# Two graph layers in one kernel: layer 0 on bf16 signs of the adjacency with one 512-column operand, row values from the diagonal, two message tables and an epilogue in three chunks

## The chip, the cores and the metric

The kernel runs on one core of a Trainium2 chip. The metric is the device time of one execution in microseconds (us). The kernel before takes 554.85 us, the median of three runs (553.38 to 556.07). A profile of one execution shows a span from the first to the last recorded instruction; the device time is longer than that span.

The engines named below are TensorE (PE in the profile, with its weight loads as PEld), VectorE (DVE), ScalarE (ACT), GpSimd (POOL) and SyncE (SP), whose queue starts most DMA transfers.

## What is computed

There are N = 2708 nodes with D = 128 features. The adjacency matrix is sparse: each row has its diagonal entry and a few neighbours, and every nonzero of a row has the same value, one over the row's degree. The first rows are the dense ones (about a hundred nonzeros), the last rows have a handful.

```python
# layer 0
XW = mobius_matvec(W, X)                       # X @ W, norms, artanh, tanh
gamma = 2.0 / max(1.0 - sum(XW * XW), EPS)
nominator   = A @ (gamma * XW)
denominator = clamp_abs(A @ (gamma - 1.0))
two_mean = nominator / denominator
AXW = mobius_scalar_mul(A.sum(-1), mobius_scalar_mul(0.5, two_mean))
x = layernorm(x + expmap0(relu(logmap0(AXW))))
# layer 1
s, d = x @ msg_w[:, :D].T, x @ msg_w[:, D:].T
messages = gelu(s[:, None, :] + d[None, :, :] + msg_b)      # for all i, j
aggregated = einsum('ijd,ij->id', messages, A)
new = concat([x, aggregated]) @ upd_w.T + upd_b
h = gelu(new) + x
x = layernorm(x + layernorm(h) * ln_w + ln_b)
```

Since messages are weighted with A, only the nonzeros of A need a message. The kernel finds them on the chip, and a dense path (behind an If, not taken with these inputs) covers matrices that have more of them than it has room for.

## The kernel before

The rows are 22 blocks of 128 nodes. The host hands over the adjacency transposed and in blocks (`adj_t`), so that one block of rows is one transfer of 1.44 MB.

*Prologue (L240 to L277).* x is transposed on TensorE block by block (L247), multiplied with W (L250), and `y` is formed: gamma times XW, gamma minus 1, and a column of ones, 130 columns per block of nodes.

*Layer 0, a loop over the blocks (L349 to L366).* SyncE starts the transfer of `aT` (L351, three buffers). ScalarE forms the signs of `aT` in bf16, `sgn` (L353); GpSimd clears the block's own diagonal in it (L355). TensorE adds up 22 f32 matmuls of `aT` with `y` in PSUM (L360), and ScalarE copies the result to `nom` (L363). `keys(b)` multiplies the signs, block by block, with a diagonal matrix of bit keys `kd` (L287, bf16), so that each nonzero leaves a number that holds its column, and VectorE takes the eight largest of each segment (MAX8, L292). `extract(l)` (L295 to L347) makes of them a list of edges: the degree of each row (L301), a running sum over the rows by a triangular matmul (L303, L304), a scan (L321), the selection matrix `R` that maps 128 edges to their rows (L311), selection matmuls (L336), and from their result the column index `J` and the flat index `F` of each edge (L344, L345). The value of each edge is then fetched from the adjacency by an indirect DMA, one for 128 edges, into `V` (L347, issued by GpSimd through the helper at L164). There are 98 tiles of 128 edges.

*Epilogue and projection (L369 to L429).* For all 22 blocks at once: norms, artanh, tanh, relu, the residual and the layer norm, as operations on 22 columns or on 2816 elements per partition on VectorE. Then block by block x is transposed (L417), projected (L420), and the d half is written to a table in DRAM (L429).

*Messages (L431 to L511).* For each block and each four tiles: GpSimd gathers the rows d_j from the table by `J` (L494, through L164; `dd`, four buffers), TensorE forms s_i with `R` (L495) and transposes `R` (L496), VectorE multiplies the transposed `R` by `V` (L498) and adds s and d (L502), ScalarE applies gelu (L503), TensorE adds up the weighted messages in `ag` (L505). The edge of a node to itself comes in with `gd` and the diagonal `dg` (L483, L484). `update` (L455) and `finish` (L462: gelu, two layer norms; the power -1/2 at L438 and three elementwise operations at L469 to L471 are on GpSimd) run for groups of 4, 4, 4, 4, 3, 2 and 1 blocks.

*Flag (L514 to L540).* Counts are compared to decide whether the dense path is needed.

Each engine executes its instructions in program order, as the Tile framework has written them down from this loop; semaphores tie engines together. PSUM banks and SBUF tiles come from pools with a fixed number of buffers, and a tile is free again when its last reader is through.

Of the kernel before, what the change touches and what calls it, by code (L numbers as in the profile page):

```python
# [10 lines left out]
F32 = mybir.dt.float32  # L11
U32 = mybir.dt.uint32
# [6 lines left out]
P = 128  # L19
BALL_EPS = 1e-5  # L20
# [3 lines left out]
MAGIC = 1597463007.0  # L24

BANK = 4
SPLIT = [[16, 8, 8, 4, 4, 1]] + [[4, 1, 1, 1, 1, 1]] * 2 + [[2, 1, 1, 1, 1, 1]] * 6 + [[1] * 6] * 13  # L30
CUTS = [[(0, 1), (1, 3), (3, 6)]] + [[(0, 6)]] * 21
TILES = [8, 6, 5, 8, 7, 5, 5, 4, 4, 4, 4, 4, 3, 3, 4, 3, 3, 3, 3, 3, 3, 3, 2, 1]
KEY = 0x5000
SPAN = 8192.0


def lists():

    out, t, c = [], 0, 0
    for b, cuts in enumerate(CUTS):  # L40
        for k0, k1 in cuts:
            n = TILES[len(out)]
            w = 8 * sum(SPLIT[b][k0:k1])
            out.append((b, range(k0, k1), c, w, t, n))
            t += n
            c += w
    return out, t, c
# [3 lines left out]
def hyperbolic_then_message_kernel(  # L51
# [3 lines left out]
    adj: bass.AP,  # L55
    adj_t: bass.AP,
    adj_d: bass.AP,
    w0: bass.AP,
# [6 lines left out]
    table: bass.AP,  # L65
# [4 lines left out]
    assert D == P and N % 2 == 0  # L70
    NB = (N + P - 1) // P
    NP = NB * P
    rows = [min(P, N - b * P) for b in range(NB)]
    full = NB if rows[-1] == P else NB - 1
    LISTS, NT, NC = lists()
    CMAX = max(v[3] for v in LISTS)
    NL = len(LISTS)
    TMAX = max(TILES)
# [4 lines left out]
    ps = ctx.enter_context(tc.tile_pool(name="ps", bufs=2, space=bass.MemoryType.PSUM))  # L83


    ident = const.tile([P, P], F32, name="ident")
    make_identity(nc, ident)
    x_sb = big.tile([P, NB, D], F32, name="x_sb")
    if full < NB:
        nc.gpsimd.memset(x_sb[:, full, :], 0.0)  # L90
    nc.sync.dma_start(x_sb[:, :full, :], x[: full * P, :].rearrange("(b p) d -> p b d", p=P))
    if full < NB:
        nc.sync.dma_start(x_sb[: rows[-1], full, :], x[full * P :, :])
    w0_sb = const.tile([P, D], F32, name="w0_sb")
    nc.scalar.dma_start(w0_sb, w0)
    mw = const.tile([P, 2 * D], F32, name="mw")
    nc.scalar.dma_start(mw, msg_w)
    uw = const.tile([P, 2 * D], F32, name="uw")
    nc.scalar.dma_start(uw, upd_w)
    mb = const.tile([P, 1], F32, name="mb")  # L100
    nc.scalar.dma_start(mb, msg_b.rearrange("(p o) -> p o", o=1))
    dg = const.tile([P, NB], F32, name="dg")
    nc.scalar.dma_start(dg, adj_d)
    rowvec = {}
    for name, src in (("ub", upd_b), ("lw", ln_w), ("lb", ln_b), ("mbr", msg_b)):
        t = const.tile([P, D], F32, name=name)
        nc.scalar.dma_start(t, bass.AP(tensor=src.tensor, offset=src.offset, ap=[[0, P], [1, D]]))
        rowvec[name] = t

# [3 lines left out]
    nhalf = const.tile([P, 1], F32, name="nhalf")  # L113
    nc.gpsimd.memset(nhalf, -0.5)
# [7 lines left out]
    loose = dict(allow_small_or_imprecise_dtypes=True)  # L122
    iota = const.tile([P, TMAX * P], F32, name="iota")
    nc.gpsimd.iota(iota, pattern=[[1, TMAX * P]], base=0, channel_multiplier=0, **loose)

    place = const.tile([P, TMAX], F32, name="place")
    nc.gpsimd.iota(place, pattern=[[P, TMAX]], base=1, channel_multiplier=1, **loose)
    nc.gpsimd.tensor_scalar(place, place, SPAN, 4096.0, op0=OP.mult, op1=OP.add)

    first = const.tile([P, NB], F32, name="first")  # L130
    nc.gpsimd.iota(first, pattern=[[P, NB]], base=0, channel_multiplier=1, **loose)
    nc.gpsimd.tensor_scalar_mul(first, first, float(N))

    key = const.tile([P, NB], I32, name="key")
    nc.gpsimd.iota(key, pattern=[[P, NB]], base=KEY, channel_multiplier=1)
    nc.vector.tensor_scalar(key, key, 16, None, op0=OP.logical_shift_left)
    kd = const.tile([P, NB, P], BF16, name="kd")
    nc.gpsimd.affine_select(
        kd,
        key.bitcast(F32).unsqueeze(2).to_broadcast([P, NB, P]),  # L140
        pattern=[[0, NB], [-1, P]],
        compare_op=OP.is_equal,
        fill=0.0,
        base=0,
        channel_multiplier=1,
    )

    wT = const.tile([P, 4, D], F32, name="wT")
    R = big.tile([P, NT, P], F32, name="R")
    J = const.tile([P, NT], U32, name="J")  # L150
    F = const.tile([P, NT], U32, name="F")
    V = const.tile([P, NT], F32, name="V")
    top = const.tile([P, NC], F32, name="top")
    deg = const.tile([P, NL], F32, name="deg")
    oe = const.tile([P, NL, 2], F32, name="oe")
    signs = const.tile([P, NB], F32, name="signs")
    cap = const.tile([P, NL], F32, name="cap")
    for l, (*_, n) in enumerate(LISTS):
        nc.gpsimd.memset(cap[:, l : l + 1], float(n * P))

    of_block = {b: [l for l, v in enumerate(LISTS) if v[0] == b] for b in range(NB)}

    def gather(o, src, at):
        nc.gpsimd.indirect_dma_start(  # L164
            out=o, out_offset=None, in_=src, in_offset=bass.IndirectOffsetOnAxis(ap=at, axis=0)
        )

    xT = big.tile([P, NP], F32, name="xT")
    mx = big.tile([P, NB, D], F32, name="mx")
    y = big.tile([P, NB, D + 2], F32, name="y")  # L170
    nom = big.tile([P, NB, D + 2], F32, name="nom")

    def bc(t):
        return t.unsqueeze(2).to_broadcast([P, NB, D])


    count = [0]

    def cols():
        count[0] += 1  # L180
        return sc.tile([P, NB], F32, name=f"c{count[0]}")

    def root(ss, least):

        a, s, q, o = cols(), cols(), cols(), cols()
        nc.vector.tensor_scalar_max(a, ss, least)
        nc.scalar.activation(s, a, AF.Sqrt)
        nc.vector.reciprocal(q, s)
        nc.vector.tensor_mul(q, q, a)
        nc.vector.tensor_add(q, q, s)  # L190
        nc.vector.tensor_scalar_mul(o, q, 0.5)
        return o

    def norm_of(v, room):
        sq = room[:, :, :D]
        nc.vector.tensor_mul(sq, v, v)  # L196
        ss = cols()
        nc.vector.tensor_reduce(ss, sq, axis=AX.X, op=OP.add)  # L198
        return root(ss, MIN_NORM * MIN_NORM)

    def artanh(n):

        z, zz, p, a, b, o = cols(), cols(), cols(), cols(), cols(), cols()
        nc.vector.tensor_scalar_min(z, n, 1.0 - BALL_EPS)
        nc.vector.tensor_mul(zz, z, z)
        nc.vector.tensor_scalar(p, zz, 1.0 / 15, 1.0 / 13, op0=OP.mult, op1=OP.add)
        for k in (11, 9, 7, 5, 3, 1):
            nc.vector.tensor_mul(p, p, zz)
            nc.vector.tensor_scalar_add(p, p, 1.0 / k)
        nc.vector.tensor_mul(p, p, z)  # L210
        nc.vector.tensor_scalar(a, z, -1.0, 1.0, op0=OP.mult, op1=OP.add)
        nc.vector.reciprocal(a, a)
        nc.vector.scalar_tensor_tensor(b, z, 1.0, a, op0=OP.add, op1=OP.mult)
        nc.scalar.activation(b, b, AF.Ln)
        nc.vector.tensor_scalar_mul(b, b, 0.5)
        nc.vector.scalar_tensor_tensor(a, z, 0.25, b, op0=OP.is_ge, op1=OP.mult)
        nc.vector.scalar_tensor_tensor(o, z, 0.25, p, op0=OP.is_lt, op1=OP.mult)
        nc.vector.tensor_add(o, o, a)
        return o

    def quotient(a, b):
        o, q = cols(), cols()
        nc.vector.reciprocal(q, b)
        nc.vector.tensor_mul(o, a, q)
        return o

    def product(a, b):
        o = cols()
        nc.vector.tensor_mul(o, a, b)
        return o  # L230

    def tanh(a, scale=1.0):
        o = cols()
        nc.scalar.activation(o, a, AF.Tanh, scale=scale)
        return o

    def bank(name, bufs=2):
        return ps.tile([P, 512], F32, name=name, bufs=bufs)

    with tc.tile_pool(name="stream", bufs=2) as stream, tc.tile_pool(name="small", bufs=2) as small:  # L240

        if full < NB:
            nc.gpsimd.memset(mx[:, full, :], 0.0)
        for b in range(NB):
            n = rows[b]
            tp = bank("mp")
            nc.tensor.transpose(tp[:, :n], x_sb[:n, b, :], ident[:n, :n])  # L247
            nc.scalar.copy(xT[:, b * P : b * P + n], tp[:, :n])
            mp = bank("kx", 3)
            nc.tensor.matmul(mp[:n, :D], lhsT=xT[:, b * P : b * P + n], rhs=w0_sb, start=True, stop=True)  # L250
            nc.scalar.copy(mx[:n, b, :], mp[:n, :D])
# [97 lines left out]
        for b in range(NB):  # L349
# [15 lines left out]
            for l in of_block[b]:  # L365
                extract(l)  # L366
# [260 lines left out]
```

## Time and profile before

| what | value |
|---|---|
| device time, median of 3 runs | 554.85 us |
| span of the profiled execution | 497.6 us |
| TensorE busy | 322.7 us (65%) |
| VectorE busy | 298.5 us (60%) |
| GpSimd busy | 242.0 us (49%) |
| ScalarE busy | 157.9 us (32%) |
| indirect gathers (V and dd) | 98 and 98, 967 and 968 ns each |
| transfer of one `aT` (1408 KB), issue to landing | 6.2 us |

A line of the profile's groups has: line of the kernel and engine, operation, output and input names with shapes, count; then busy time in us and the mean of one in ns; then idle time of the engine just before these instructions, and what ended it. A line of the waits has: engine, name and line, what it waited for; the total in us, the number of times, the longest.

The page cuts the span into 40 slices of 12.4 us; each digit is the busy share of a slice in tenths:

```profile
PE   1681998999999999997000058566582657657700
DVE  2629486676867767767989983422240537545751
ACT  1953142536455355451260225311120112111200
POOL 3200077778556354343000000677777878787441
PEclk9999997999999999999555559778887779586955
```

Layer 0 is in slices 5 to 18, the epilogue and projection in 19 to 25, the messages after that.

### The profile page before, as it was taken

What the parts mean: (1) busy time and instruction counts of PE and PEld (TensorE: products, weight loads), DVE (VectorE), ACT (ScalarE), POOL (GpSimd) and SP (SyncE); (2) the same over time, 40 slices, a digit from 0 to 9 for tenths busy, and PEclk for the clock granted to TensorE, in tenths of its full rate; (3) what the DMA queues carried; (4) which work ended last, traced back from release to release, by engine and by line L of the source; (5) the groups of instructions that cost most, each with busy time, mean ns of one, the idle gap of its engine ahead of it and who ended that gap; (6) DMA issues with size and microseconds to landing.
All of it is one profiled execution on the core that took longest, in us unless ns stands there. A gap on an engine that the chain in (4) does not pass through costs nothing.

```text
span 497.6 us, 7268 instructions
## 1 busy us (share of the span) xinstructions
PE 322.7 (65%) x2506; PEld 298.9 (60%) x2506; DVE 298.5 (60%) x965; ACT 157.9 (32%) x321; POOL 242.0 (49%) x321
## 2 busy tenths in 40 slices
PE   1681998999999999997000058566582657657700
PEld 1560997999999999996000046465572656657500
DVE  2629486676867767767989983422240537545751
ACT  1953142536455355451260225311120112111200
POOL 3200077778556354343000000677777878787441
PEclk9999997999999999999555559778887779586955
DMA  8600333355545546500000002111211121212000
GB/s 261 246 1 1 113 123 118 118 174 185 224 151 201 212 148 226 204 32 0 1 0 0 0 22 84 45 54 53 53 51 53 35 71 32 68 30 57 23 28 3
DMA packets 17718, 43.54 MB, mean 87 GB/s; under 512 B 6180, under 2 KB 12620, under 8 KB 14860
## 3 DMA queue, kind: packets, MB, share of 16 engines
q1 hardware_dynamic: 10108, 35.94, 20.1%
q0 software_dynamic: 6272, 6.49, 5.5%
q10 hardware_dynamic: 1296, 0.60, 0.5%
q8 instruction: 21, 0.34, 0.3%
q14 instruction: 21, 0.17, 0.1%
HBM read 40.18 MB, written 2.83 MB: 86 GB/s over the span
## 4 chain that ended last, share of the span: by engine, by line
PE 41%; POOL 18%; DVE 18%; issue 8%; ACT 6%; DMA 5%; ACTq 1%; POOLq 0%; DVEq 0%
PE mp L360 22%; POOL dd L164 12%; PE sel L336 5%; PE kx L287 5%; DMA dd<-table_dram,J 4%; PE kx L420 3%; POOL rs L438 2%; ACT sgn L353 2%; DVE c L198 2%; PE kx L250 2%; POOL v L469 1%; POOL v L470 1%; DVE y L196 1%; DVE top L292 1%; PE sel L304 1%
## 5 line engine op out<-in xcount | busy, mean ns | idle before, releaser
L164 POOL DMA_INDIRECT dd<-table_dram,J x98 | 94.9, 968 | 94.8 <-DMA table_dram<-nom 66.4
L164 POOL DMA_INDIRECT V<-in_adj_dram,F x98 | 94.8, 967 | 93.6 <-DVE F L345 57.7
L360 PE MATMUL mp<-y,aT 128*128 128x130 f32 x968 | 134.3, 286 | 3.4 <-ACT sgn L353 3.4
L360 PEld LDWEIGHTS mp<-y,aT 128*128 128x128 f32 x968 | 120.1, 196 | 3.7 <-ACT sgn L353 3.7
L292 DVE MAX8 top<-kx 128x8 f32<-128x512 f32 (+4 forms) x179 | 85.5, 512 | 6.5 <-PE kx L287 6.3
L353 ACT ACTIVATE sgn<-aT 128x2816 bf16<-128x2816 f32 x22 | 56.1, 2552 | 67.1 <-PE kx L287 56.5
L287 PE MATMUL kx<-kd,sgn 128*128 128x128 bf16 x484 | 44.8, 225 | 9.5 <-DVE top L292 9.5
L495 PE MATMUL kx<-y,R 128*128 128x128 f32 x196 | 40.2, 326 | 7.0 <-DVE dd L502 6.1
L287 PEld LDWEIGHTS <-sgn 128*128 128x128 bf16 x484 | 36.4, 103 | 11.8 <-DVE top L292 9.2
L503 ACT ACTIVATE ge<-dd 128x512 f32<-128x512 f32 (+3 forms) x30 | 16.6, 552 | 79.9 <-DVE dd L502 64.9
L496 PE MATMUL kx<-ident,R 128*128 128x128 f32 x98 | 25.7, 323 | 22.8 <-DVE rw L498 15.0
L505 PE MATMUL ag<-rw,ge 128*128 128x128 f32 x196 | 35.3, 333 | 7.2 <-DVE dw L483 3.1
L495 PEld LDWEIGHTS kx<-y,R 128*128 128x128 f32 x196 | 34.3, 236 | 8.8 <-DVE dd L502 7.6
L417 PE MATMUL mp<-ident,x_sb 128*128 128x128 f32 x22 | 5.1, 317 | 50.3 <-DVE x_sb L413 50.3
L502 DVE TENSOR_TENSOR dd<-kx,dd 128x512 f32<-128x512 f32 (+3 forms) x30 | 17.5, 582 | 33.0 <-DMA dd<-table_dram,J 27.7
L505 PEld LDWEIGHTS ag<-rw,ge 128*128 128x128 f32 x196 | 31.6, 242 | 8.9 <-ACT ge L503 8.6
L417 PEld LDWEIGHTS mp<-ident,x_sb 128*128 128x128 f32 x22 | 3.5, 161 | 52.0 <-DVE x_sb L413 50.4
L336 PE MATMUL sel<-z,R 128*128 128x49 f32 (+3 forms) x196 | 28.0, 288 | 7.7 <-DVE R L311 4.5
L336 PEld LDWEIGHTS sel<-z,R 128*128 128x128 f32 x196 | 25.3, 202 | 9.2 <-issue 5.0
L496 PEld LDWEIGHTS kx<-ident,R 128*128 128x128 f32 x98 | 15.0, 168 | 25.0 <-DVE rw L498 15.9
L321 DVE TENSOR_TENSOR_SCAN scan<-m,oe 128x48 f32<-128x48 f32 (+3 forms) x24 | 8.8, 367 | 30.4 <-ACT oe L305 30.3
L458 PE MATMUL sel<-wT,xT 128*128 128x128 f32 x44 | 11.3, 351 | 19.0 <-DVE h L460 19.0
(165 smaller groups left out, 518.5 us busy)
## 6 DMA issues: line engine op xcount, KB each, us to landing
aT<-in_adj_t_dram SPq DMA_DIRECT2D x22, 1408.0 KB, 6.2
V<-in_adj_dram,F POOLq DMA_INDIRECT x98, 2.4
dd<-table_dram,J POOLq DMA_INDIRECT x98, 2.5
table_dram<-nom SPq DMA_DIRECT2D x22, 64.0 KB, 1.5
out_dram<-h SPq DMA_DIRECT2D x21, 64.0 KB, 1.6
mw<-in_L_gnn_msg_w_dram ACTq DMA_DIRECT2D x1, 128.0 KB
uw<-in_L_gnn_upd_w_dram ACTq DMA_DIRECT2D x1, 128.0 KB
w_sb<-in_L_gnn_W_dram ACTq DMA_DIRECT2D x1, 64.0 KB, 1.8
```

The costliest lines, as they stand in the source:

```text
L164: nc.gpsimd.indirect_dma_start(out=o, out_offset=None, in_=src, in_offset=bass.IndirectOffsetOnAxis(ap=at, axis=0))
L287: nc.tensor.matmul(kp[:, i * P : (i + 1) * P], lhsT=sgn[:, j, :], rhs=kd[:, j, :], start=True, stop=True)
L292: nc.vector.max(top[:, c : c + 8], seg[:, s, :])
L336: nc.tensor.matmul(sp[:, k, :], lhsT=R[:, t0 + k0 + k, :], rhs=z, start=True, stop=True)
L353: nc.scalar.activation(sgn, aT, AF.Sign, accum_out=signs[:, b : b + 1])
L360: nc.tensor.matmul(op[:, : D + 2], lhsT=aT[:, j, :], rhs=y[:, j, :], start=(j == 0), stop=(j == NB - 1))
L420: nc.tensor.matmul(dp[:, : 2 * D], lhsT=x1T[:, b * P : (b + 1) * P], rhs=wT[:, 0:2, :].rearrange("p a d -> p (a d)"), start=True, stop=True,)
L495: nc.tensor.matmul(X[:, k, :], lhsT=R[:, t, :], rhs=s_nm[:, b, :], start=True, stop=True)
L496: nc.tensor.transpose(RT[:, k, :], R[:, t, :], ident)
L502: nc.vector.tensor_tensor(dd[:, :w, :], X[:, :w, :], dd[:, :w, :], op=OP.add)
L503: nc.scalar.activation(ge[:, :w, :], dd[:, :w, :], AF.Gelu)
L505: nc.tensor.matmul(ag[:, :P], lhsT=ge[:, k, :], rhs=rw[:, k, :], start=False, stop=(k0 + k == t1 - 1))
```

## The change

Blocks have 124 rows now (22 x 124 = 2728). The three limbs of y (bf16 parts whose sum is y; 3 x 129 columns), a column of ones and 124 key columns (block j has the key 2^j) make one operand of 512 bf16 columns. One matmul for each pair of blocks, signs with this operand, gives sums, count and keys together. Since the nonzeros of a row all have the row's diagonal value, the sums of signs are scaled by the diagonal; that the values do equal the diagonal is counted on VectorE over the whole matrix. The gather of V is gone. The epilogue and the projection run in three chunks of blocks, after blocks 10, 19 and 21, and the messages are split by the half of the nodes from which they come: table 0 holds blocks 0 to 10, table 1 the others. All early messages (table 0) of all blocks come first, then the late ones with update and finish, in groups of two blocks. x arrives already transposed beside its normal layout. `layer0` is the sums, signs and the comparison of one block; `batch` is the list making of `extract` for several blocks at once (peeling the keys of a word one after another, MAX8, degrees, columns, triangular matmuls, scan, R, selection, J); `factors` is some 35 small operations on the columns of a chunk, one artanh among them; `power` and `gather` are on GpSimd. The `layer0` matmul with `nidentb` takes the block's own key away. The flag's counts and the dense path are adapted. Names with limbs: `hi`, `mid`, `lo`.

```diff
-SPLIT = [[16, 8, 8, 4, 4, 1]] + ...
-TILES = [8, 6, 5, 8, 7, ...]
+CUT = 11
+CHUNKS = [(0, 11), (11, 20), (20, 22)]
+BATCHES = [((0,), 0), ((1,), 8), ((2, 3, 4), 4), ((5, 6, 7, 8, 9), 2), ((10, 11, 12, 13), 2),
+           ((14, 15, 16, 17, 18), 1), ((19, 20, 21), 1)]
+EARLY = [5, 5, 4] + [6, 5, 4, 4, ...]
+LATE = [2, 2, 2] + [3, 2, 2, 2, ...]
...
+    def layer0(b, store):
+        dgb = stream.tile([Q, Q], F32, name="dgb", bufs=2)
+        nc.sync.dma_start(dgb, ...)
+        sgn = stream.tile([Q, NB, Q], BF16, name="sgn")
+        for h in range(2):
+            aT = stream.tile([Q, HALF, Q], F32, name="aT", bufs=3)
+            nc.sync.dma_start(aT, adj_t[b, :, h * HALF : (h + 1) * HALF, :])
+            at = 2 * b + h
+            nc.scalar.activation(sgn[:, ...], aT.bitcast(U32), AF.Sign, accum_out=nn[:, at : at + 1])
+            nc.vector.scalar_tensor_tensor(aT, aT, 1.0, dgb...to_broadcast([Q, HALF, Q]),
+                op0=OP.mult, op1=OP.is_equal, accum_out=ne[:, at : at + 1])
+        op = bank("op")
+        for j in range(NB):
+            nc.tensor.matmul(op[:Q, :WIDE], lhsT=sgn[:, j, :], rhs=ym[:, j, :], ...)
+            if j == 0:
+                nc.tensor.matmul(op[:Q, KEYS:WIDE], lhsT=nidentb[:Q, :Q], rhs=ym[:, b, KEYS:], ...)
+        nc.vector.tensor_reduce(nom[:, b, :], op[:Q, :ONES]..., axis=AX.X, op=OP.add)
+        nc.scalar.copy(cnt[:, b : b + 1], op[:Q, ONES : ONES + 1])
+        nc.scalar.activation(junk, nom[:, b, :D], AF.Square, accum_out=ss[:, b : b + 1])
...
+        for s, (lo, hi) in enumerate(segments(v.shape[2])):
+            nc.vector.max(v[:, i, s, :], words[:, lo:hi])
+            nc.vector.max_index(idx[:, i, s, :], v[:, i, s, :], words[:, lo:hi])
...
+    def peel(v, pid, keys, levels, shape):
+        for k in range(levels):
+            nc.vector.tensor_scalar(hi, v.bitcast(I32), 0x7F800000, None, op0=OP.bitwise_and)
+            nc.vector.tensor_tensor(keys(k), hi, pid, op=OP.bitwise_or)
+            if k + 1 < levels:
+                nc.vector.tensor_sub(v, v, hi.bitcast(F32))
...
+    def batch(blocks, S, v, idx):
...
+        limbs([zl[:, i]... for i in range(3)], scan, cmf)
...
+                nc.scalar.activation(r0[:, ...], iota[...], AF.Abs, scale=2.0, bias=mid[...])
+                nc.vector.tensor_scalar(R[:, t0 : t0 + nt, :]..., r0..., dflat..., -0.5, ...)
...
+                        nc.tensor.matmul(sp[:, q, :], lhsT=R[:, t, :], rhs=zl[:, h, k, i, :], ...)
+    def factors(b0, b1, dgc, den, cntc, ssc):
...
+    def epilogue(b0, b1, dgc, cntc, store):
+        f = factors(b0, b1, ...)
+        for b in range(b0, b1):
+            nc.scalar.activation(v, v, AF.Relu, scale=f[:, b - b0 : b - b0 + 1])
+            nc.scalar.activation(junk, v, AF.Square, accum_out=us[:, b : b + 1])
...
+        power(un, un, 0)                    
+        nc.scalar.activation(g, un, AF.Tanh)
...
+        for b in range(b0, b1):
+            nc.vector.scalar_tensor_tensor(v, v, g[...], x_sb[:, b, :], op0=OP.mult, op1=OP.add)
+            nc.vector.bn_stats(st, v)
+            nc.vector.bn_aggr(mv[:, b, :], st)
+        power(rs, rs, 1)
...
+        for b in range(b0, b1):
+            nc.scalar.activation(x_sb[:, b, :], nom[:, b, :D], AF.Identity, scale=rs..., bias=nm...)
+            nc.tensor.transpose(tp[:, :Q], x_sb[:, b, :], ident[:Q, :Q])
+            nc.scalar.copy(x1T, tp[:, :Q])
+            store(b, x1T)
+    def project(b, x1T):
+        dp = bank("op")
+        nc.tensor.matmul(dp[:Q, :], lhsT=x1T, rhs=wall..., start=True, stop=False)
+        nc.tensor.matmul(dp[:Q, :], lhsT=first3, rhs=bias..., start=False, stop=True)
+        nc.scalar.copy(d, dp[:Q, D : 2 * D])
+        nc.sync.dma_start(tables[k][at * Q : (at + 1) * Q, :], d)
+        limbs([sl[:, b, i, :] for i in range(3)], dp[:Q, :D], tmp)
+        nc.scalar.copy(own1[:, b, :], dp[:Q, 2 * D : 3 * D])
+        nc.scalar.activation(gd[:Q, b, :], dp[:Q, 3 * D :], AF.Gelu)
+    def messages(b, k):
...
+            dd = edge.tile([P, 4, D], F32, name="dd", bufs=3)
+                gather(dd[:, i, :], tables[k], J[:, t : t + 1])
+                for h in range(3):
+                    nc.tensor.matmul(X[:, i, :], lhsT=R[:, t, :], rhs=sl[:, b, h, :], ...)
+                nc.tensor.transpose(RT[:, i, :Q], R[:, t, :], identb[:Q, :Q])
+            nc.scalar.copy(rw[:, :w, :], RT[:, :w, :Q])
+            nc.vector.tensor_tensor(dd[:, :w, :], X[:, :w, :], dd[:, :w, :], op=OP.add)
+            nc.scalar.activation(ge[:, :w, :], dd[:, :w, :], AF.Gelu)
...
+        if k == 0:
+            nc.scalar.copy(gd[:, b, :Q], ag[:, :Q])
...
-        GROUPS = [(0, 4), (4, 4), (8, 4), (12, 4), (16, 3), (19, 2), (21, 1)]
+    for b in range(NB):
+        layer0(...)
+        if b in ends:
+            batch(blocks, S, v, idx)
+        for b0, b1 in CHUNKS:
+            if b == b1 - 1:
+                epilogue(b0, b1, dg, cnt, project)
+    for b in range(NB):
+        messages(b, 0)
...
+    GROUPS = [(b, min(2, NB - b)) for b in range(0, NB, 2)]
+    for b0, n in GROUPS:
+        for b in range(b0, b0 + n):
+            update(h[:, b - b0, :], messages(b, 1), b, dg[:, b : b + 1])
+        finish(h, b0, n)
```

Line numbers of the kernel after that the prediction uses: the comparison L352, the matmuls of layer 0 L363, the selection L492, the helper of the gathers L325.

## The prediction, made before the changed kernel ran

> **What bounds the kernel now.** I read the page's 40 slices first, then a table of stages, then the waits, then the chain that ended last. The table: stage from:to, its length, then busy time and instruction count of each engine, the granted clock, the DMA share and rate.
>
> ```profile
> 50.00:127.00 77.00, 73.83 (x661) 72.35 (x662) 51.42 (x162) 28.56 (x47) 49.90 (x64) 0.96 0.41 144
> 127.00:234.60 107.60, 104.96 (x1058) 103.16 (x1056) 78.33 (x235) 50.23 (x82) 52.97 (x76) 1.00 0.43 154
> 234.60:314.00 79.40, 21.59 (x96) 16.55 (x96) 65.58 (x223) 25.48 (x66) 0.94 (x1) 0.61 0.06 19
> 314.00:458.40 144.40, 89.13 (x541) 81.57 (x542) 58.51 (x183) 23.92 (x48) 113.72 (x114) 0.77 0.19 50
> ```
>
> Columns after the length are PE, PEld, DVE, ACT, POOL. Blocks 0 to 10, then 11 to 21 (layer 0): TensorE is full, 74 of 77 and 105 of 107.6 us; VectorE is at 67% and 73%. Then 79.4 us of epilogue and projection, alone on VectorE and ScalarE. Then the messages, where GpSimd has 114 of 144 us.
>
> ```profile
> POOL dd L164 <- DMA table_dram<-nom: 66.4, 1, 66.4
> ACT sgn L353 <- PE kx L287: 56.5, 16, 7.9
> POOL dd L164 <- issue: 23.5, 83, 0.3
> ```
>
> Line, whom it waited for, total, times, longest. The first message gather waits for the whole epilogue. The signs wait for matmuls, so ScalarE has slack in layer 0. From one gather to the next there is 0.3 us besides the gather itself, so a gather costs 1.25 us of GpSimd:
>
> ```profile
> L164 POOL DMA_INDIRECT dd<-table_dram,J x98 | 94.9, 968 | 94.8 <-DMA table_dram<-nom 66.4 <-issue 23.5 <-DMA dd<-table_dram,J 1.8
> L164 POOL DMA_INDIRECT V<-in_adj_dram,F x98 | 94.8, 967 | 93.6 <-DVE F L345 57.7 <-issue 20.9 <-DVE bad L515 12.4
> L438 POOL TENSOR_TENSOR rs<-ve,nhalf 128x4 f32<-128x4 f32 x8 | 8.4, 1047 | 3.9 <-DVE ve L448 3.8
> L438 POOL TENSOR_TENSOR rs<-ve,nhalf 128x2 f32<-128x2 f32 x2 | 1.4, 701 | 2.1 <-DVE tot L538 1.1 <-DVE ve L448 1.0
> L502 DVE TENSOR_TENSOR dd<-kx,dd 128x512 f32<-128x512 f32 x15 | 10.3, 687 | 26.3 <-DMA dd<-table_dram,J 20.9 <-PE sel L459 3.7 <-PE kx L495 0.8
> L292 DVE MAX8 top<-kx 128x8 f32<-128x512 f32 x97 | 65.1, 688 | 3.3 <-PE kx L287 3.1
> ```
>
> Of the two gathers of each tile, the V one already hides below TensorE. The page's chain agrees: PE 41%, POOL 18%, DVE 18%.
>
> [...] L287 issues 7 in 0.55 us and 4 in 0.39, 53 ns each; the granted clock is 0.61 in the epilogue. [...] I bound the pair with its maximum between one and three MAX8 passes (0.3 to 0.85 us at 128 columns, 285 ns measured for one) and take 0.4 for the mostly narrower segments.
>
> **The change part by part.** The profiled execution's span is 497.6 us; the median of the runs, 554.85, lies 57.2 above. I keep 57.2 around the new span.
>
> *Start.* The 22 transposes with their ScalarE copies (275 and 266 ns a pair) go; 12 limb copies and subtracts come (about 0.65 us each). Net shorter: I take block 0's sum complete at 46 us, against 57.3 now (first L360 at 50.0).
>
> *Layer 0, TensorE.* Out go 44 L360 instructions at 0.11 us (18 in 2.23, 4 in 0.67), the 22 key matmuls at 0.055, and a 49-column f32 selection: 7.5 us a block in the steady part (180.3 to 187.75). In come 22 [...] plus one small: 4.8 us, and 327 bf16 selection matmuls in all at about 0.06, some 20 us. TensorE alone would need 22 x 4.8 + 26 = 132 us instead of 185.
>
> *Layer 0, VectorE.* The added comparison with the diagonal (after's L352) is 44 passes of 1364 elements: [...] 1.58 us, plus 0.08 for the accumulator: 1.66 each, 73 us in all. A reduce of 387 adds 0.56 a block. The MAX8 of L292 (85.5 us on the page) are replaced by 46 pairs and by short MAX8 in the batches. For blocks 0 to 10: 20 compares 33, reduces 6, pairs 12, batch 0 with six peel levels and 31 MAX8 about 20 (small dependent operations follow each other at 0.215 us), batches 1 and 2 about 8.5 and 11: 91 us, and 6 of waits. In program order nothing covers it: the next batch of comparisons stands behind the batch chains on VectorE, and TensorE's queue has block 3's matmuls behind batch 0's selection. So 97 us, VectorE-bound: block 10 done at 46 + 97 = 143, while now block 10 is done at 127. Blocks 11 to 19: 3.3 + 0.6 + about 1.4 for pairs and the uncovered part of the batches = 5.3 a block, x9 = 48.
>
> *V gathers removed.* 98 x 1.25 us of GpSimd, all beside TensorE's layer 0: worth nothing by itself. Only where message gathers are put in their place does it pay. In the order of instructions only 12 of 109 stand before the end of layer 0, because dd has three buffers and the gelu that frees them stands on ScalarE after the last chunk.
>
> *Epilogue in 3 chunks.* ScalarE's queue has chunks 1 and 2 in one stretch without a Sign between, and the projection shares the two PSUM banks of layer 0's sums, so block 11's matmuls wait for almost all of chunk 1. The chunk is thus serial, not hidden. Chunk 1 (11 blocks): VectorE factors, about 35 small operations with the table load for Ln and the batch that is interleaved, 22; Relu and Square 11 x 0.59 = 6.5; pow (0.385 + 0.165 a column, from 1047 and 701 ns: 2.2) and tanh with its table load (1.3), 3.6 with what is small; multiply-add and statistics 11 x 0.49 = 5.4; second pow and two small operations 2.5; normalise, transpose, copy, project, four copies and gelu, ScalarE-bound, 11 x 1.7 + 3.5 = 22. Sum 62. Chunk 2 (9 blocks) by the same terms 54; blocks 20 and 21 then 10; chunk 3 to the first gelu of a message 17. The eleven table writes of chunk 1 stand on SP before a half block of 14; they are short (64 KB, 1.5 us) and cost a wait only if the halves are late.
>
> So layer 0 without chunks is 46 + 97 + 48 + 10 = 201, the chunks 133: messages run freely from 334 us, against 314 now.
>
> *Messages.* 62 early gathers remain: x 1.25 = 78, to 412. TensorE and VectorE have less to do than now (row value no longer multiplied in; R in bf16), so GpSimd is the pace. Late part: 35 gathers, and 11 groups each with two GpSimd adds (0.72 at 256 columns) and two pow at 0.70. h has two buffers, so a group starts when the one before last is through: about 10.2 us for two groups. 17 gathers and the first add 22; five pairs of groups 51; the last tail 9: 82, to 494. Last computation to span end is now 8.4; I take 7: 501. Dearest uncounted: the ring of three half blocks is held by the comparison[...]; I add 5% of the 150 us after block 0, 7. Span 508, time 508 + 57 = 565.
>
> Covers that could fail: the transfer of a half block (6.2 us for a whole one now, so about 3) is hidden by two halves in flight; if the comparison runs late on VectorE, each costs some 2 us, 44 in all up to 35 us, taken at 7. [...]
>
> **The rivals.**
>
> *Faster, 527.* One mechanism: VectorE's work of blocks 0 to 10 runs beside the batch chains' waits, because those chains stall on TensorE and ScalarE and comparisons fill the stalls. Layer 0 then goes at TensorE's 4.8 us plus selection, and blocks 0 to 10 take 70 us, not 97; chunk 1's factors fall beside the batch (-11). 565 - 27 - 11 = 527. For it: VectorE has 17 us idle at the scan L321 alone now. Against: the order on each queue is fixed, and 91 us are busy time, not waits. It decides if block 10 is done before about 116 us or the factors cost under 10.
>
> *No change, 555.* Same path, but the ring costs nothing (-7) and messages begin some 3 us earlier. A gain of layer 0 that exactly pays for the exposed chunks.
>
> *Much slower, 600.* The half-block ring turns into the bound: three buffers of half a block cover one and a half blocks only, against three whole ones now, and each is free only after the comparison. At 44 x 0.8 us exposed latency +35. For it: VectorE is behind by the batch chains. Against: 3 us a half is less than the work on it (2 x 1.66 per block beside 4.8).
>
> *Doing less than it says.* "Two tables" is to let gathers begin early, but with 12 of 74 placed in layer 0 only 15 us of GpSimd time is moved forward. That is inside the forecast.
>
> **How the numbers follow.** Forecast (565, own range 558 to 585) 0.45; much slower 0.20; no change 0.13; faster 0.22. About 0.5% (2.8 us) is what a measurement of this kernel can tell from none. The range 530 to 602 leaves out the lower half of the faster case and the upper half of the much slower one, 0.1 each. Faster 0.22, same 0.13, slower 0.65.
>
> **What would show it.** Comparison near 1.66 us x44; block 10's sums at about 143 us; a hole of some 50 to 60 us in TensorE's matmuls between blocks 10 and 11, another between 19 and 20; first free-running gathers near 334; gathers at 1.25 us after that; late part near 82. Wrong if the comparison is half as long, if Signs of block 11 run within chunk 1, or if the gathers start before 310.

## The result and the profile after

The kernel after takes 699.5 us (median of four runs, 698.6 to 700.6) against 555.3 us before: 1.262 times, interval 1.257 to 1.267. Forecast were 565 us, with 602 as the upper end of the range.

The page of the kernel after, its busy tenths and transfer rate in 40 slices of 17.4 us:

```profile
span 697.3 us, 6473 instructions
...
PE   4000827165771105854664410776655465676620
DVE  4247658464543643243443454245110111246551
ACT  2016423221512465531233144726222232343320
POOL 9100000000000212070000011004656646586641
...
DMA  5222111222222210142222210000211212121100
GB/s 144 87 104 103 57 69 45 101 85 103 105 98 105 103 72 7 35 98 102 105 103 103 98 46 0 22 12 19 51 37 43 46 30 47 38 54 31 30 24 17
```

The same two rows of the kernel before, in slices of 12.4 us, with layer 0 in slices 5 to 18:

```profile
DMA  8600333355545546500000002111211121212000
GB/s 261 246 1 1 113 123 118 118 174 185 224 151 201 212 148 226 204 32 0 1 0 0 0 22 84 45 54 53 53 51 53 35 71 32 68 30 57 23 28 3
```

In layer 0 of the kernel after (slices 5 to 23) no compute engine is full for long, while the transfer rate stands at 98 to 105 GB/s over whole stretches. Before, the same loop moved up to 226 GB/s in a slice. The DMA row says 2 tenths at the ceiling of the kernel after: about a quarter of the 16 engines' time, not all of it. So something limits the transfers that is not the engines' time in sum.

The groups of the kernel after, with count, busy time, mean in ns, idle time before and its releaser:

```profile
L363 PE MATMUL op<-ym,sgn 124*124 124x512 bf16 x484 | 140.9, 453 | 55.6 <-DVE idx L384 33.0 <-DVE hi L390 14.9 <-DVE m L429 6.5
L325 POOL DMA_INDIRECT dd<-table_dram,J x109 | 106.7, 979 | 87.7 <-ACT ge L613 29.2 <-issue 26.0 <-DMA table_dram<-d 25.3
L352 DVE SCALAR_TENSOR_TENSOR aT<-aT,dgb 124x1364 f32<-124x1364 f32 x44 | 69.3, 1574 | 102.5 <-ACT sgn L349 61.9 <-ACT cnt L373 40.7
L349 ACT ACTIVATE sgn<-aT 124x1364 bf16<-124x1364 uint32 x44 | 58.9, 1339 | 236.0 <-DMA aT<-in_adj_t_dram 210.3 <-issue 15.2 <-PE op L363 10.4
```

The signs (L349), which waited for matmuls before (56.5 us), now wait 210 us for the half blocks themselves, and the comparison (L352) waits for the signs. So the half blocks look like the cause and the comparison's wait like an echo; the experiments below test that. The comparison costs about what the prediction gave it, 1.574 us and 0.08 for the accumulator.

The stretches of the kernel after (from and to; length; busy PE, PEld, DVE, ACT, POOL; granted clock, DMA share, GB/s), cut where blocks 0, 10, 11, 19 had their sums, then at the first gelu of a message and at the first group's finish:

```profile
80.40:226.00 145.60, 74.99 (x398) 45.95 (x396) 80.11 (x307) 43.92 (x96) 1.65 (x6) 0.72 0.23 86
226.00:296.50 70.50, 27.50 (x143) 14.89 (x144) 30.36 (x155) 37.31 (x135) 10.28 (x8) 0.65 0.15 55
296.50:399.10 102.60, 55.93 (x230) 31.79 (x228) 41.04 (x120) 29.20 (x67) 13.30 (x14) 0.76 0.29 102
...
478.40:607.60 129.20, 74.73 (x555) 66.50 (x553) 20.20 (x57) 36.69 (x106) 76.25 (x81) 0.72 0.18 41
```

In the first and third line no engine has much more than half of the stretch, and 102 GB/s take 0.29 of the engines' time.

The kernel before takes 555 us in some sessions of measurement and 499 us in others, so each number below is marked kind 555 or kind 499 by what the kernel before took beside it, and numbers are compared within one kind. The profile before, with a span of 497.6 us, is of kind 499, while the timed runs beside it are of kind 555; in both kinds the device time is the recorded span plus 1.7 to 2 us. Some expectations below put the difference down to the chip. Both kinds were measured on chip number 3, so the chip alone doesn't make the kind.

### The profile page after: what moved, and what is told of

Read it like the earlier page. It is cut to its first block, busy times and chain, and to the rows that moved or that the text cites. A ratio compares the mean times of both kernels' runs of the same rounds, so it can differ in the third digit from the quotient of the medians.

```text
span 697.3 us, 6473 instructions
## 1 busy us (share of the span) xinstructions
PE 322.7 (46%) x1787; PEld 224.3 (32%) x1787; DVE 288.1 (41%) x1121; ACT 235.5 (34%) x677; POOL 177.8 (26%) x339
## 5 line engine op out<-in xcount | busy, mean ns | idle before, releaser
L363 PE MATMUL op<-ym,sgn 124*124 124x512 bf16 x484 | 140.9, 453 | 55.6 <-DVE idx L384 33.0
L349 ACT ACTIVATE sgn<-aT 124x1364 bf16<-124x1364 uint32 x44 | 58.9, 1339 | 236.0 <-DMA aT<-in_adj_t_dram 210.3
L325 POOL DMA_INDIRECT dd<-table_dram,J x109 | 106.7, 979 | 87.7 <-ACT ge L613 29.2
L352 DVE SCALAR_TENSOR_TENSOR aT<-aT,dgb 124x1364 f32<-124x1364 f32 x44 | 69.3, 1574 | 102.5 <-ACT sgn L349 61.9
L363 PEld LDWEIGHTS <-sgn 124*124 124x124 bf16 x484 | 75.6, 163 | 109.5 <-issue 71.2
L615 PE MATMUL ag<-rw,ge 128*128 128x124 f32 x218 | 47.2, 360 | 8.3 <-ACT rw L610 7.3
L605 PE MATMUL sel<-sl,R 124*128 124x128 bf16 x327 | 42.0, 273 | 9.9 <-DVE dd L612 9.4
L605 PEld LDWEIGHTS <-R 124*128 124x128 bf16 x327 | 32.2, 128 | 16.0 <-issue 14.7
L492 PE MATMUL sel<-zl,R 124*128 124x16 bf16 (+4 forms) x327 | 17.6, 197 | 33.8 <-ACT zl L298 12.7
L575 PE MATMUL op<-wall,x1T 128*124 128x512 f32 x44 | 29.4, 756 | 6.9 <-ACT x1T L569 6.8
L608 PE MATMUL rt<-identb,R 124*128 124x124 bf16 x109 | 22.1, 272 | 20.5 <-DVE R L476 8.9
L492 PEld LDWEIGHTS <-R 124*128 124x128 bf16 x327 | 15.5, 113 | 37.2 <-DVE R L476 29.1
L473 ACT ACTIVATE r<-iota,mid 124x256 f32<-124x256 f32 (+5 forms) x48 | 23.9, 531 | 3.1 <-DVE R L476 2.7
```

What stands on the lines that cost most here:

```text
L325: nc.gpsimd.indirect_dma_start(out=o, out_offset=None, in_=src, in_offset=bass.IndirectOffsetOnAxis(ap=at, axis=0))
L349: nc.scalar.activation(sgn[:, h * HALF : (h + 1) * HALF, :], aT.bitcast(U32), AF.Sign, accum_out=nn[:, at : at + 1])
L352: nc.vector.scalar_tensor_tensor(aT, aT, 1.0, dgb.unsqueeze(1).to_broadcast([Q, HALF, Q]), op0=OP.mult, op1=OP.is_equal, accum_out=ne[:, a ...
L363: nc.tensor.matmul(op[:Q, :WIDE], lhsT=sgn[:, j, :], rhs=ym[:, j, :], start=(j == 0), stop=(j == NB - 1))
L473: nc.scalar.activation(r0[:, : nt * P], iota[:Q, : nt * P], AF.Abs, scale=2.0, bias=mid[:, k * n + i : k * n + i + 1])
L492: nc.tensor.matmul(sp[:, q, :], lhsT=R[:, t, :], rhs=zl[:, h, k, i, :], start=(h == 0), stop=(h == 2))
```

## The experiments

### 128 partitions instead of 124

The profile's DMA share from block 11's sum to block 19's in the kernel after, 0.29 of 16 engines, is 4.6 engines' time on average, with the gathers in it. The traces don't name engines, but they have the start and the duration of each packet of a transfer, so that the packets in flight at one time can be counted. Transfers of 124, 125, 128 and of 112 and 12 partitions show how that count goes with the partitions.

`pad_at` and, in the other kind, `pad_at_again`:

```diff
-            aT = stream.tile([Q, HALF, Q], F32, name="aT", bufs=3)
-            nc.sync.dma_start(aT, adj_t[b, :, h * HALF : (h + 1) * HALF, :])
+            aT_all = stream.tile([P, HALF, Q], F32, name="aT", bufs=3)
+            nc.sync.dma_start(aT_all, adj_t[b, :, h * HALF : (h + 1) * HALF, :])
+            aT = aT_all[:Q]
```

with `adj_t` laid out with 128 rows per block, the last four of zeros.

> The kernel after, with one change: each half block of the adjacency is loaded as 128 partitions (four rows of zeros that nothing reads) instead of 124. Theory A (the 124-partition transfer uses few DMA engines and its rate bounds layer 0): a half block lands in about 3 us instead of 6 to 7, ScalarE's 210 us of waiting for aT nearly vanish, time 570 to 600 us. Rival B (the ring of three halves, held by the comparison, sets the pace): the transfers start no earlier, time above 680 us. Rival C (VectorE's batch chains set the pace, the waits for aT are only their echo): above 670 us.

> The kernel after, unchanged, beside the other three of this call on one chip. The loss against the kernel before in the same call: if the transfers' engines are the cause on any chip, after_again is 120 to 150 us slower than pad_at_again, whatever the kernel before takes here.

> pad_at once more, beside after_again and the kernel before. 120 to 150 us below after_again. On a chip where the kernel before takes 555 us: 1.03 of it. On one where it takes 500 us: 1.08 to 1.10 of it, since the kernel before lost 55 us on the other chips and the kernel after, whose layer 0 has other waits, less.

Measured: 572.0 us (kind 555; 1.031 of before, interval 1.027 to 1.036). In kind 499: after_again 669.3 and pad_at_again 542.5 us (1.088 of before). The padding is worth 127.5 us in one kind and 126.8 in the other. It costs 3% more bytes. ScalarE's wait for half blocks fell from 210 to 75 us in pad_at, less far than "nearly vanish". Of theory A it holds that the rate of the 124-partition transfers bounds layer 0; on how many DMA engines they run is not shown. B and C as the main cause fall.

`after_125` pads to 125 rows, `after_112_12` adds no byte:

```diff
-            nc.sync.dma_start(aT, adj_t[b, :, h * HALF : (h + 1) * HALF, :])
+            nc.sync.dma_start(aT[:112], adj_t[b, :112, h * HALF : (h + 1) * HALF, :])
+            nc.sync.dma_start(aT[112:], adj_t[b, 112:, h * HALF : (h + 1) * HALF, :])
```

> The kernel after, with each half block loaded as 125 partitions (one row of zeros that nothing reads). Theory A [...]: a quarter more rate, a half block in about 5.2 us instead of 6.5, time 625 to 660 us, between 699.5 and pad_at's 572. If it is the alignment of the rows, or a size that 128 happens to meet, 125 partitions do not help: above 690 us.

> The kernel after, each half block loaded by two transfers, 112 partitions and 12, without a byte added. Theory A: [...] as pad_at, 565 to 585 us. If it is the number of partitions in all that counts, 690 us or more.

Measured, both in kind 499: 630.5 and 546.5 us, against 669.3 with 124 partitions and 542.5 with 128. One row more gives 39 us. The prices of both expectations were worked out from the 699.5 and 572 us of kind 555; that 125 partitions would give a quarter more rate and 112 with 12 as much as 128 was the author's estimate. Against kind 499 the order is what they had right: 125 partitions lie between 124 and 128, and 112 with 12 is as fast as 128. From block 0's sum to block 10's it took 146.3 us with 124, 126.7 with 125, 90.3 with 112 and 12, 90.5 with 128.

The packets settle it. Of the time from block 11's sum to block 19's in which SyncE's queue has any packet in flight, it has four during 84% in the kernel after, and five during 81% in after_125. In pad_x_again (128 partitions, below) the number goes up to 16 and a few more. A packet (one partition's 5456 bytes) takes the same in all three, a median of 211, 211 and 209 ns. In after_112_12 the number goes as high as with 128 partitions, though a packet takes a median of 312 ns there. Four such packets at a time are 4 x 5456 bytes in 211 ns, or 103 GB/s, and five are 129 GB/s; the pages show 102 to 105 and 123 to 133. So with 124, 125 and 128 partitions the number of partitions changes how many packets go at once, and not how fast each one goes. In layer 0 of the profile before (128 partitions, 11264 bytes each) 16 are in flight during 50% of such time, more often than any other number. Why it is four, five and 16 is not shown.

`before_124` puts the cost into the kernel before:

```diff
-            nc.sync.dma_start(aT, adj_t[b])
+            nc.sync.dma_start(aT[:124], adj_t[b, :124])
+            nc.sync.dma_start(aT[124:], adj_t[b, 124:])
```

> The kernel before with each transfer of a block split in two, 124 partitions and 4 partitions. Theory A: the transfer of a block takes about 12 to 13 us instead of 6.2, and layer 0 goes at that pace (22 x 12.8 = 282 us instead of 185): time 635 to 665 us. Rivals B and C: below 565 us, since nothing else is changed. It also shows how the recorded span of a kernel of this form stands to its device time (497.6 and 554.85 us in the profile before).

Measured, kind 555: 629.0 us in the fastest of four runs, 638.8 to 642.0 in the others. The fastest is 73 us above the kernel before (555.8) and 6 us below the forecast range. The page of its profile stands at 100 to 108 GB/s over most of layer 0, again with four packets in flight, each of 11264 bytes and 424 ns (422 in the profile before). So the kernel before slows down by the same cause, without any other part of the change.

### What the comparison and the diagonal's transfer add

> The kernel after with 124-partition transfers, without the comparison with the diagonal on VectorE and without the transfer of the diagonal (the check that all values of a row equal its diagonal is left out). A half block is then freed by ScalarE alone and VectorE has 73 us less. Theory A: transfers stay at their rate, time 685 to 700 us. Rival B: 620 to 650 us. Rival C: 630 to 660 us.

> The kernel after with 124-partition transfers, where VectorE compares with a constant tile instead of the diagonal, so that the 22 small transfers of the diagonal are gone and the comparison's time stays (the check of the values is left out; its count is not used). after_no_compare was 34 us faster than after, with blocks 0 to 10 in 123.7 us instead of 145.7. If the transfers of the diagonal on the same few engines cost that, blocks 0 to 10 take 123 to 128 us here; if the comparison does, by holding a half block's buffer, 140 to 146 us.

The first removes L352 and the transfer at L343, the second only the transfer (`dgb = ones[:Q, :Q]`). Measured: after_no_compare 665.4 us (kind 555), 34 less than the kernel after and in none of the three ranges; after_compare_constant 654.4 (one run, kind 499), 15 less than after_again. Theory A had allowed 15 for leaving out the comparison, so this is a miss: transfers of 124 partitions are not all. From block 0 to 10: 145.6 us with both (146.3 in after_again), 139.2 with the comparison alone, 123.7 with neither, or 6.2 us for each of 20 half blocks. So of 22 us in this stretch about 15.5 are the comparison and 6.4 the diagonal's transfer in the same queue. What SyncE's queue waits for at the transfer of a half block, first in after_no_compare, then in after_compare_constant:

```profile
SPq L345 <- DMA aT<-in_adj_t_dram: 170.8, 34, 11.5
```

```profile
SPq L346 <- DVE aT L351: 85.1, 12, 24.6
```

Without the comparison, a transfer waits for an earlier transfer; with it, it waits for the comparison (L351 there), which holds the buffer until VectorE gets to it. So rival B exists, with a share of this size.

> The kernel with 128-partition half blocks, without the comparison and the transfer of the diagonal (the check of the values is left out). If VectorE's comparison is the next bound of layer 0, as the prediction has it, it is 40 to 73 us faster than with the comparison: 515 to 550 us. If TensorE or the batch chains are the next bound, it is less than 15 us faster.

With 128 partitions, leaving both out gives 533.8 us (kind 555), 38 less than pad_at (0.959 of before, interval 0.954 to 0.964), just below the forecast of 40 though inside the range of times. The 22 transfers of the diagonal are gone here too, so at most half of the comparison's 73 us stands in the path.

### The start, the writes and the chunks

`pad_x_and_diagonal` loads x and the diagonal as 128 partitions too; `pad_x_again` repeats it; `pad_writes_split` also splits each table write into 112 and 12 rows.

```diff
-    x_sb = big.tile([Q, NB, D], F32, name="x_sb")
-    nc.sync.dma_start(x_sb, x_p)
+    x_sb_all = big.tile([P, NB, D], F32, name="x_sb")
+    nc.sync.dma_start(x_sb_all, x_p)
+    x_sb = x_sb_all[:Q]
...
-        dgb = stream.tile([Q, Q], F32, name="dgb", bufs=2)
+        dgb_all = stream.tile([P, Q], F32, name="dgb", bufs=2)
...
```

> As pad_at, and x and the diagonal of each block are loaded as 128 partitions too. Theory A: x then lands some 15 us earlier, block 0's sums are complete near 55 us instead of 69, and the 22 small transfers take less of the queue: 550 to 562 us. If the start is set by the chain of small operations on VectorE instead, less than 5 us is gained.

> pad_x_and_diagonal once more: 20 to 28 us below pad_at_again on any chip (546 of 572 before).

> As pad_x_and_diagonal, with each write of the table as two transfers, 112 rows and 12. If the slow writes hold up the copies in the projection (their buffer is free only when the write has landed), the chunks get shorter by up to 10 us. If not, the extra transfers on SyncE cost 0 to 3 us.

Measured: 546.4 us in kind 555, 25.6 less than pad_at and below the forecast range of 550 to 562, and 0.988 of the kernel before (interval 0.984 to 0.991); 520.1 in kind 499, 22.4 less than pad_at_again, and 1.043 of before. In kind 499 block 0's sum comes at 50.6 us instead of 71.3, and blocks 0 to 10 take 87.8 us instead of 90.5, so that most of the gain is x at the start. Splitting the writes: 520.7 in kind 499, no difference.

`pad_one_chunk` is pad_at with `CHUNKS = [(0, 22)]`; `pad_all_one_chunk` is the same on pad_x_and_diagonal, and `pad_one_chunk_again` repeats that one.

> As pad_at, with one chunk of 22 blocks after layer 0 instead of three. The three chunks stand with some 128 us in the trace of pad_at (65, 50 and 13.5). If they are serial and each pays its fixed chain again, one chunk costs about 100 us by the prediction's terms, and the 12 early gathers that now stand among layer 0 (15 us of GpSimd) move behind it: 545 to 562 us. If the chunks pay by letting messages begin early, it is slower than pad_at, above 575 us.

> As pad_x_and_diagonal, with one chunk of 22 blocks. If the gain of one chunk (14 us at pad_at) is independent of the start, 528 to 540 us, faster than pad_x_and_diagonal's 546.4 and than the kernel before. If the transfers of the start gave the chunks room that one chunk doesn't have, no gain.

> pad_all_one_chunk once more: 10 to 30 us below pad_x_again, and below the kernel before on either kind of chip.

Measured: pad_one_chunk 557.7 us in kind 555, 14 less than pad_at and 1.008 of the kernel before; pad_all_one_chunk and its repeat 493.3 and 492.1 us in kind 499, 27 to 28 less than pad_x_again, and 0.987 and 0.988 of the kernel before (interval of the repeat 0.983 to 0.993). The range of 528 to 540 was meant for kind 555, in which this version was not run. The stretch from block 21's sum to the first gelu in pad_one_chunk_again, and the two chunk stretches with blocks in between in pad_x_again (columns as above):

```profile
214.00:295.60 81.60, 28.72 (x128) 14.89 (x125) 32.14 (x178) 46.17 (x194) 18.99 (x11) 0.69 0.06 16
```

```profile
138.40:205.00 66.60, 27.12 (x143) 14.84 (x144) 30.38 (x155) 37.44 (x135) 10.33 (x8) 0.67 0.17 53
205.00:254.90 49.90, 42.66 (x230) 25.82 (x228) 40.67 (x120) 28.90 (x67) 16.36 (x14) 0.97 0.77 225
254.90:327.70 72.80, 33.32 (x198) 20.39 (x199) 36.63 (x213) 39.81 (x139) 6.49 (x6) 0.70 0.05 16
```

One chunk of 22 blocks takes 82 us, less than the 100 expected; chunk 1 of 11 blocks alone takes 67 us, up to the next block's sum, so half the blocks don't cost half the time: each chunk pays a fixed chain again. The middle line is layer 0 as it was meant: 225 GB/s, VectorE 41 of 50 us, TensorE 43.

### More buffers for the gathered rows

> As pad_one_chunk, with eleven buffers for the gathered rows (in the memory of the 512-column operand, which is free after layer 0) instead of three. If the three buffers pace the early messages (125 us for 62 gathers in the trace, where 1.25 us each gives 78), that part falls to 80 to 95 us and the time is 30 us or more below pad_one_chunk. If the chain of TensorE, ScalarE and VectorE for each group of tiles paces them, less than 10 us is gained.

```diff
-            dd = edge.tile([P, 4, D], F32, name="dd", bufs=3)
+            dd = wide[:, ring[0] % 11 * 4 * D : (ring[0] % 11 + 1) * 4 * D].rearrange(...)
```

Measured: 562.0 us (kind 555) against 557.7: no gain. The waits for the gelu that frees a buffer were not the pace. Kind 499 shows what is. The messages of table 0 and the first two blocks of table 1 (79 gathers, up to the first group's finish) in pad_x_again and, of the same instructions, in after_again:

```profile
327.70:428.10 100.40, 70.21 (x562) 61.19 (x560) 20.16 (x58) 36.19 (x109) 76.27 (x81) 0.83 0.23 53
```

```profile
478.40:578.70 100.30, 73.15 (x565) 63.55 (x564) 20.09 (x58) 35.99 (x108) 76.24 (x81) 0.80 0.23 53
```

In 100 us there are 76 us of gathers with 0.3 us between them: 1.25 us each without a hole, so GpSimd is the pace and three buffers are enough. The kernel after, in kind 555, took 129 us for it (the last line of its stretches above) with the same busy time. The traces show where the holes begin. The last packet of a gather ends 2.2 us after the gather's start in both kinds (medians of after and after_again). But VectorE's addition, which needs the gathered rows, starts 0.5 us after that packet in after_again and 2.6 us after it in the kernel after (medians of the additions in this stretch; 0.5 us in pad_x_again and 2.9 in pad_x_and_diagonal). So in kind 555 the rows arrive as early after their gather starts, and the engine that uses them goes on later. What holds it up is not shown.

### The kernel before, once more

> The kernel before, unchanged, profiled once more. The profile before had a span of 497.6 us at a mean clock of 0.836, while the spans of the timed runs are 552 to 557 us at 0.79 to 0.81. If that profiled execution was an unusual one, the span is now 552 to 558 us, and the stage that is longer tells where the 55 us lie; a lower granted clock alone would make layer 0 longer and leave the messages, which GpSimd paces, as they were.

Measured: 555.4 us, span 553.7. Layer 0 and the messages are longer, the epilogue not (83.4 us in both from block 21's sum to the first message gather). A lower clock alone is thus not the cause, since by the expectation it would have left the messages as they were. One stretch of layer 0, in the profile before and in before_again:

```profile
97.90:142.00 44.10, 43.94 (x444) 43.16 (x442) 32.13 (x96) 20.68 (x34) 31.22 (x44) 1.00 0.52 180
```

```profile
97.90:142.00 44.10, 32.36 (x253) 30.25 (x253) 19.28 (x54) 13.29 (x23) 23.81 (x32) 0.85 0.29 99
```

The same 44 us hold 444 matmuls in one and 253 in the other. Block 21's sum is copied at 230.6 and at 265.3 us, the first message gather starts at 314 and 348.7: 35 us in layer 0, 31 of them by block 9, and the remaining 21 in the messages and what follows them. So the profile from which the prediction was worked out is not an unusual execution but one of kind 499.

## Why the prediction was wrong

Its points, beside the kernel after and beside the kernel whose large loads have 128 partitions (both kind 499, like the profile that the prediction was worked out from), in us from the span's start:

| point | prediction | after_again | pad_x_again |
|---|---|---|---|
| block 0's sum | 46 | 80.7 | 50.6 |
| block 10's sum | 143 | 227.0 | 138.4 |
| block 19's sum | 253 | 400.0 | 254.9 |
| block 21's sum | 317 | 465.4 | 314.3 |
| first gelu of a message | 334 | 478.4 | 327.8 |
| first group's finish (412 + 22) | 434 | 578.7 | 428.1 |
| last computation | 494 | 656.8 | 506.1 |
| span | 508 | 668.2 | 517.6 |

- The step that failed stands under "Covers that could fail": a half block's transfer "(6.2 us for a whole one now, so about 3) is hidden by two halves in flight". It carried the duration over from 128 partitions to 124. With 124 a half takes 6.2 us where nothing else holds it (after_no_compare), with the comparison and the diagonal's transfer 7.3 (145.6 us for 20), against 4.4 us of work (87.8 us for the same 20 in pad_x_again). A transfer of 124 partitions had four packets in flight where one of 128 had up to 16 and more. The place of the "much slower" rival was right and its price, 35 us, was not: it priced an exposed latency, where the rate had fallen. 127 us are shown for the half blocks and 22 to 26 for x and the diagonal. The prediction also priced this delay in two ways: 2 us for each of 44 would be 88 us, and its 35 us are 0.8 us for each.
- The diff had the number 124 in every tile, and the prediction asked of the transfers only whether they were hidden.
- "I keep 57.2 around the new span" was wrong as well. Around every span there are 1.7 to 2 us; the 57 were the difference between the two kinds. The kernel after, with no V gathers in layer 0, is about 30 us longer in kind 555 (669.3 to 699.5), not 57, and 29 of these lie in the stretch of the early messages (100.3 and 129.2 us). Without this term's surplus the forecast would have been near 540 (508 + 1.7 + 30), further from the result; that the wrong term brought it nearer is luck.
- The comparison: 1.66 us forecast, 1.574 + 0.082 measured. The profile before gives the same estimate: two-tensor operations of 512 and 2816 columns took 687 ns (L502) and 3092 (L377), on a straight line 1.58 us for 1364, and reading an accumulator took 83 ns (L301). The reduce of 387 columns: 0.56 forecast, 0.551 measured. A maximum with its index: 0.4 taken, 0.51 measured (the maximum 0.209 and two instructions for the index of 0.085 and 0.220, medians). VectorE as the bound of blocks 0 to 10: 97 us forecast, 87.8 with transfers of 128 partitions, and 79 of them busy. Chunk 1: 62 forecast, 66.6 with block 11's sum in it. Blocks 11 to 19: 48 and 49.9. The chunks are serial, as forecast.
- Early messages: 100 us to the first finish, as forecast (78 + 22). The groups after it were mis-sized: 60 us forecast (10.2 for two groups and a tail of 9), 78 measured in pad_x_again, 7.2 a group and a tail of 6. From the last computation to the end it is 11.5 us, not 7. The 7 us added for what was uncounted, the shorter blocks 0 to 10 and an earlier first gelu cover part of that, so that the forecast span of 508 lies within 10 us of pad_x_again's 517.6 in part because errors cancel.
- The faster rival (VectorE's work in the batch chains' stalls) does not occur: with transfers of 128 partitions blocks 0 to 10 take 88 us, not 70. Its support was read too high: VectorE's wait at the scan L321 is 11.5 us in the stretch of blocks 0 to 10 and 30.3 us in all, not 17. The rival's 4.8 us a block for TensorE was the author's estimate; with the selection TensorE was busy for 42.7 us in the 8 blocks from block 11's sum to block 19's, at a granted clock of 0.97 (pad_x_again).
- That pad_x_and_diagonal beats the kernel before in kind 555 (0.988) and not in kind 499 (1.043) goes with the third point: from kind 499 to kind 555 the kernel before loses 56 us and pad_x_and_diagonal 26.

The last version, one chunk and 128 partitions, was measured in kind 499 alone. There it takes 1.2% less than the kernel before and 26% less than the kernel after.

## What to carry to other kernels

When a change alters a tile's partitions, ask of each of its transfers how many packets it still has in flight and at what rate it then moves, before asking whether it is hidden: here 124 partitions had four packets in flight and 128 up to 16 and more, and four rows of padding were worth 127 us. In this case the sign of it was a rate that stood flat at 102 to 105 GB/s while the DMA share was 0.29. And compare the profiled span with the timed runs first: if they differ by more than the few us around a span, the profile is of another condition than the times.

## What the runs showed of the hardware that was not expected

A transfer of 124 partitions moved 102 to 105 GB/s in the kernel after (100 to 108 in before_124, with larger packets), one of 125 moved 123 to 133, and one of 128 moved 225 GB/s over a whole stretch of the same loop (256 in its best slice), where other work was the bound. The packets in flight were four, five and up to 16 and more; one of 5456 bytes took 0.21 us in each case.

The same kernel before took 555 us in some sessions and 499 us in others. The parts that grew are those in which GpSimd gathers (layer 0 and messages before, the early messages after), while layer 0 of the kernel after, which has few gathers, agreed within 1 us in both (block 19's sum at 399.1 and 400.0 us). In the early messages the packets of a gather ended as soon in both kinds, 2.2 us after its start, and the addition that uses its rows followed 0.5 us later in kind 499 and 2.6 to 2.9 us later in kind 555. Why it follows later, and whether the same holds for the longer layer 0 of the kernel before, stays open.
